# Projecting the image prompts' keys and values together in two 32-column weight tiles

## The chip, the cores and the metric

The kernel runs on one core of one Trainium2 chip. The metric is device time in microseconds (us) of one execution. Three runs of the kernel before took 433.48, 433.68 and 434.69 us; their median is 433.68 us. Engines are named as in the profile: PE is the matrix engine, PEld its weight loads, DVE the vector engine, ACT the scalar engine, POOL the general engine, and SP the engine whose queue issues the transfers (DMAs).

## The reference

There are 8 batches. In each, 112 query rows of 320 channels attend, with 20 heads of 16 channels, to a context of 375 rows of 512 channels. The last 4 rows of every context are image prompts; the other 371 are text.

```python
text_ehs = encoder_hidden_states[:, :-NUM_TOKENS]        # 371 rows
ip_ehs = encoder_hidden_states[:, -NUM_TOKENS:]          # 4 rows
q = heads(hidden_states @ W_q)
k_t, v_t = heads(text_ehs @ W_k), heads(text_ehs @ W_v)
probs_t = softmax(q k_t^T * attn_scale)
text_out = probs_t v_t
k_ip, v_ip = heads(ip_ehs @ W_k_ip), heads(ip_ehs @ W_v_ip)
attn_scores = q k_ip^T * attn_scale
qsem = l2norm(probs_t text_ehs);  sem = qsem l2norm(ip_ehs)^T
probs_ip = softmax(attn_scores + 0.5 * sem) * spatial_mask
out = (text_out + probs_ip v_ip) @ W_out + b_out + hidden_states
```

Only `k_ip` and `v_ip` concern the change: the 4 prompt rows of all 8 batches, 32 rows of 512 channels, times two weight matrices of 512 by 320. They are computed once for all batches.

## The kernel before

The 20 heads of a batch go in five steps of four heads. One batch has five steps, and `steps` lists all forty. The main loop goes through them in pairs (`pair`, or `alone` for the first), and after each pair `behind(n)` does what is left between: the Gram matrix, keys, values and queries of the next batch, and the end of the batch before. The order on PE, SP and DVE, and in the loop on ACT and POOL too, is the order in which the program is written. Nothing is moved by a planner.

A step runs like this. Scores (`ps_s`) are a product of keys `kT` and queries `qm` on PE, 32 channels of contraction for each head. DVE takes their maximum (`nmx`, L645), ACT the exponential (`p`, L649). SP's queue sends `p` to a rearranged buffer `xg` (L658), and DVE transposes 32x32 blocks of that into `xgT` (L672). PE multiplies `xgT` with the batch's matrix `u` into `ps_qd` (L683), four heads side by side, each in its own 32 rows of the array. ACT (L710) and DVE (L743) read the result. Scores are made two steps ahead: within the pair of steps 1 and 2, PE also makes those of step 3, in PSUM banks of the pools `sc` and `mm` (two banks each), and the first products of step 2 use these same four banks. So they wait until ACT's `p` of step 3 has read them.

PSUM banks come from three pools (`qd` 4, `sc` 2, `mm` 2 banks). `bank(name)` takes the pool that the list `turn` names next, and `behind` fills that list.

The prompts: `normalised_prompts` transposes the 32 prompt rows into `ipT` (128 partitions, 4 chunks of the contraction, 32 prompts). `wip` holds both prompt weight matrices; SP's queue loads them with `load_embed` behind the transfers of step 1, and then loads `x`, `W_out` and the bias. `prompt_projections` is a generator; `run` advances it piece by piece.

- L267, in `behind(0)`: `spread` on POOL (L123, L124) moves the last 64 of the keys' weight columns apart, so that each head of 16 channels is followed by 16 zeros.
- L268 to L278: for each of three blocks of 128 key channels, four matmuls (`ps_kip`) with the weights standing in the array (128x128) and the 32 prompts streaming through. ACT copies the result into `kip` (channels on partitions), and DVE makes `kipb`, keys masked by head, for batch 0.
- L285 to L292: four matmuls (`ps_vip`) the other way round: 32 prompts stand as weights in 32 columns, 320 value columns stream. ACT copies them into `vip`.
- L295, in `behind(2)`: `vip` goes to DRAM. Later batches fetch their four rows from there.

`kip` is read by POOL in `keys(b)` (L476), which puts the prompts' keys behind the text's keys, first for batch 1 in `behind(2)`. `kipb` is read by `prompt_logits` in `behind(4)`. `k3` is a buffer in which heads 16 to 19 stand 32 channels apart with zeros between; batch 1 uses it first in `behind(2)`, when its values are done.

On PE each float32 matmul of the program appears as two weight loads and two matmul instructions; a transpose appears as one of each.

Of the kernel before, what the change touches and what calls it, by code (L numbers as in the profile page):

```python
# [8 lines left out]
F32 = mybir.dt.float32  # L9
# [11 lines left out]
def kernel(  # L21
# [14 lines left out]
    nc = tc.nc  # L36
    P = 128
    B, S, C = x.shape
    T, E = ehs.shape[1:]
    H = HEADS  # L40
    D = C // H
# [3 lines left out]
    NE = E // P  # L45
    HC = P // D
    NC = (C + P - 1) // P
    CP = NC * P
    FULL = C // P
# [7 lines left out]
    N = B * NIP  # L57
# [18 lines left out]
    work = ctx.enter_context(tc.tile_pool(name="work", bufs=2))  # L76
# [6 lines left out]
    turn = []  # L83
    pools = {"mm": ps_mm, "sc": ps_sc, "qd": ps_qd}

    def bank(name, spare=False):

        tag = turn.pop(0) if turn else "sc" if spare else "mm"
        return pools[tag].tile([P, 512], F32, tag=tag, name=name)
# [12 lines left out]
    wv_sb = const.tile([P, NE, C + REST], F32, tag="wv_sb", name="wv_sb")  # L102

    wip = work.tile([P, UCOL], F32, tag="u", name="wip")
    wkip_sb = wip[:, : NE * CP].rearrange("p (e f) -> p e f", f=CP)
    wvip_sb = wip[:, NE * CP : NE * (CP + C)].rearrange("p (e f) -> p e f", f=C)
    wo_sb = const.tile([P, NC, C], F32, tag="wo_sb", name="wo_sb")
    ip_sb = const.tile([N, E], F32, tag="ip_sb", name="ip_sb")
    sm_sb = const.tile([S, 1], F32, tag="sm_sb", name="sm_sb")
# [9 lines left out]
    def spread(eng, t):  # L119

        v = t[:, :, FULL * P :].rearrange("p k (a r d) -> p k a r d", r=2, d=D)
        for a in (3, 2, 1):
            eng.tensor_copy(v[:, :, a, 0, :], v[:, :, a // 2, a % 2, :])  # L123
        eng.memset(v[:, :, :, 1, :], 0.0)  # L124
# [43 lines left out]
    ident = const.tile([P, P], F32, tag="ident", name="ident")  # L168
# [38 lines left out]
    k3 = const.tile([P, NT, GROUP, 2, D], F32, tag="k3", name="k3")  # L207
# [7 lines left out]
    ipT = const.tile([P, NE, N], F32, tag="ipT", name="ipT")  # L215
    ipnT = const.tile([P, NE, N], F32, tag="ipnT", name="ipnT")
    kip = const.tile([P, NC, N], F32, tag="kip", name="kip")

    kipb = const.tile([P, NC, HC, NIP], F32, tag="kipb", name="kipb")
    vipd = dram.tile([N, C], F32, tag="vipd", name="vipd", bufs=1)  # L220
# [43 lines left out]

    def prompt_projections():

        spread(nc.gpsimd, wkip_sb)  # L267
        for i in range(NC):  # L268
            ps = bank(f"ps_kip{i}")
            for e in range(NE):  # L270
                nc.tensor.matmul(
                    ps[:, :N],
                    wkip_sb[:, e, i * P : (i + 1) * P],
                    ipT[:, e, :],
                    start=(e == 0),
                    stop=(e == NE - 1),
                )
            nc.scalar.copy(kip[:, i, :], ps[:, :N])  # L278
            nc.vector.tensor_tensor(
                kipb[:, i],  # L280
                kip[:, i, :NIP].unsqueeze(1).to_broadcast([P, HC, NIP]),
                hmask.unsqueeze(2).to_broadcast([P, HC, NIP]),
                ALU.mult,
            )
            yield  # L285
        ps = bank("ps_vip")
        for e in range(NE):
            nc.tensor.matmul(
                ps[:N, :C], ipT[:, e, :], wvip_sb[:, e, :], start=(e == 0), stop=(e == NE - 1)
            )  # L290
        vip = work.tile([N, C], F32, tag="vip", name="vip", bufs=1)
        nc.scalar.copy(vip, ps[:N, :C])  # L292
        yield

        nc.sync.dma_start(vipd, vip)  # L295
        yield


# [165 lines left out]
    def gram_to_groups(b, blocks):  # L464

        for q in blocks:
            for a in range(GROUP):
                nc.sync.dma_start(
                    st[b]["u"][a * RG : (a + 1) * RG, q * GW : (q + 1) * GW],
                    ug[q * RG : (q + 1) * RG, :],  # L470
                )
# [543 lines left out]
    def run(key, make, pieces=1):  # L1015

        if key not in gens:
            gens[key] = make()
        for _ in range(pieces):
            next(gens[key], None)  # L1020
# [58 lines left out]
    def k(b, pieces=1):  # L1079
        run(("k", b), lambda: keys(b), pieces)  # L1080
# [104 lines left out]
    def behind(n):  # L1185

        b, g = steps[n]
        nb = b + 1
        two = steps[n + 1 : min(n + 3, len(steps) - NG + 1)]

        def tr(i):
            if i < len(two):
                transposed(*two[i], 0, BLK // (1 + i))

        if b % 2 == 0 and g == 0:
            if n == 0:
                turn[:] = ["sc", "sc", "mm", "qd", "qd", "qd", "qd", "mm"]
            else:
                turn[:] = ["qd"] * 4 + ["mm"]
                k(b)  # L1200
                f(b - 1)
                if b - 1 < B - 2:
                    prompt_values(b - 1)
            gr(nb)
            tr(0)
            gr(nb)
            if n:
                f(b - 1)
            gr(nb)
            if n == 0:  # L1210
                run(("pp",), prompt_projections, NC + 1)
            v(nb)
            tr(1)
            if n:
                f(b - 1, 2)
            load_next(b + 2)
        elif b % 2 == 0 and g == 2:
            turn[:] = ["qd"] * 6 + ["mm"]
            gram_to_groups(nb, (2,))
            k(nb)  # L1220
            q(nb, 3)
            tr(0)
            v(nb)
            q(nb)
            v(nb)
            if b == 0:
                run(("pp",), None)
            tr(1)
            values_to_dram(nb, nc.sync)
        elif b % 2 == 0:  # L1230
            new = nb < B - 1
            turn[:] = ["qd"] * (3 + (b > 0)) + (["qd", "mm", "mm"] if new else ["mm"])
            turned(b + 2)
            q(nb, 1 + (not new))
            if b > 0:
                f(b - 1)
            else:
                run(("t", b), lambda: prompt_logits(b))
            k(nb)
            tr(0)  # L1240
            if b > 0:
                f(b - 1)
            if new:
                gr(nb + 1, 3)
            tr(1)
            if b > 0:
                f(b - 1)
            load_next(b + 3)
            if new:
                f(b)  # L1250
                prompt_values(b)
        elif g == 1:
            turn[:] = ["qd"] * 4 + ["mm"]
            gram_to_groups(nb, (2,))
            q(b)
            k(b)
            k(nb)
            tr(0)
            f(b - 1)
            v(nb)  # L1260
            tr(1)
            v(nb)
            f(b - 1, 3)
            values_to_dram(nb, nc.sync, 0, 2)
            if b == B - 3:
                prompt_values_by_head()
        else:
            turn[:] = ["qd"] * 3 + ["sc"]
            v(nb)
            f(b - 1)  # L1270
            values_to_dram(nb, nc.sync, 2)
            tr(0)
            k(nb)
            f(b - 1, 2)
            tr(1)
            values_to_groups(nb)
        assert not turn, (b, g, turn)

    for n in range(0, len(steps) - NG, 2):
# [4 lines left out]
        b, g = steps[n]  # L1284
# [16 lines left out]
    b = B - 1  # L1301
# [12 lines left out]
    for g in range(NG):  # L1314
# [20 lines left out]
        if g < NG - 1:  # L1335

            n = GROUP - 1 if g <= LEAD else 1
# [89 lines left out]
```

## Time and profile before

| What | Before |
|---|---|
| Median of three runs | 433.68 us (433.48 to 434.69) |
| The profiled execution's own time | 434.62 us |
| Its span, first to last instruction | 432.9 us |
| PE busy | 423.2 us (98%) |
| DVE, ACT, POOL busy | 328.5, 190.7, 112.1 us |
| Mean granted PE clock over the span | 0.995 |

The profiled execution has 1.7 us outside its span. In the page, the second part cuts the span into 40 slices of 10.8 us. A row of the timeline gives start, duration, engine, line, operation, output<-input, shapes, the number of instructions merged, and in brackets the idle time ahead with what ended it. A PE shape such as `128*32` gives the rows and columns of the array in use, and `128x320` after it the partitions and streamed columns. A row of grouped instructions gives the busy time, in which overlaps count once, and the mean duration of one. The duration of a PE instruction includes the time until its result has left the array, so that a stream's own pace is read from starts.

### The profile page before, as it was taken

How to read it: one execution, taken by the hardware profiler on the slowest of the kernel's cores; microseconds unless marked ns; L12 is line 12 of the kernel's file. 1: busy time of each engine (PE TensorE's matmuls, PEld its weight loads, DVE VectorE, ACT ScalarE, POOL GpSimd, SP SyncE). 2: the span in 40 equal slices, each digit the busy share in tenths (PEclk: the TensorE clock that was granted, in tenths of full speed). 3: DMA queues.
4: the chain of work that ended last, by engine and by line, in shares of the span. 5: the costliest groups of instructions: out<-in, count | busy, mean ns of one | idle time of the engine just before them, and what ended most of it. 6: DMA issues, size and time to landing. Idle time of an engine off the chain costs nothing. (4 is left out here: it accounts for less than half of the span.)

```text
span 432.9 us, 12985 instructions
## 1 busy us (share of the span) xinstructions
PE 423.2 (98%) x5024; PEld 323.8 (75%) x5024; DVE 328.5 (76%) x687; ACT 190.7 (44%) x649; POOL 112.1 (26%) x270
## 2 busy tenths in 40 slices
PE   8999999999999999999999999999999999999986
PEld 8756677778686887778686887778776888776783
DVE  4045467797899897796889898787888897778884
ACT  2264123334553454333643464233633563346793
POOL 4302200012151234012142126002133226026440
PEclk9999899999999999999999999999999999999999
DMA  8669946487554566576744466575755436663300
GB/s 243 171 173 248 213 112 154 143 192 155 148 142 123 157 160 150 152 177 138 181 134 124 127 171 159 144 187 134 173 160 145 111 101 166 175 157 100 101 4 27
DMA packets 57931, 64.21 MB, mean 148 GB/s; under 512 B 18368, under 2 KB 52024, under 8 KB 57870
## 3 DMA queue, kind: packets, MB, share of 16 engines
q1 hardware_dynamic: 57304, 62.66, 57.2%
q8 instruction: 40, 0.66, 0.7%
q10 hardware_dynamic: 566, 0.72, 0.5%
q14 instruction: 21, 0.17, 0.1%
HBM read 18.67 MB, written 5.32 MB: 55 GB/s over the span
## 5 line engine op out<-in xcount | busy, mean ns | idle before, releaser
L683 PE MATMUL ps_qd<-u,xgT 32*112 32x232 f32 (+11 forms) x3840 | 215.4, 352 | 1.9 <-POOL u L599 1.9
L683 PEld LDWEIGHTS ps_qd<-u,xgT 32*112 32x112 f32 x3840 | 180.0, 172 | 36.5 <-issue 8.1
L672 DVE STREAM_TRANSPOSE xgT<-xg 128x768 f32<-128x768 f32 (+1 forms) x63 | 121.2, 1951 | 9.2 <-DMA xg<-p 9.1
L649 ACT ACTIVATE p<-ps_s,nmx 112x371 f32<-112x371 f32 x160 | 85.8, 586 | 52.5 <-DVE nmx L645 48.5
L743 DVE CUSTOM_DVE_ANT_0 junk<-ps_qd,p 112x371 f32<-112x371 f32 x148 | 80.2, 542 | 31.5 <-ACT pvs L710 11.4
L645 DVE TENSOR_REDUCE nmx<-ps_s 112x1 f32<-112x371 f32 x160 | 77.3, 537 | 28.0 <-PE ps_s L632 26.0
L599 POOL COPY u<-vr 128x64 f32<-128x64 f32 x120 | 26.7, 237 | 192.9 <-PE ps_qd L683 116.4
L526 PE MATMUL ps_v<-wv_sb,ctxT 128*128 128x384 f32 (+1 forms) x192 | 63.5, 477 | 0.3 <-ACT kT L499 0.3
L632 PE MATMUL ps_s<-kT,qm 32*112 32x375 f32 (+1 forms) x320 | 61.9, 487 | 1.0 <-ACT shared L728 0.7
L526 PEld LDWEIGHTS ps_v<-wv_sb,ctxT 128*128 128x128 f32 x192 | 35.4, 190 | 20.7 <-ACT kT L499 1.2
L710 ACT COPY pvs<-ps_qd 112x21 f32<-112x21 f32 x150 | 21.4, 200 | 62.2 <-DVE ss L743 61.0
L492 PE MATMUL ps_k<-ctxT,wk_sb 128*128 128x371 f32 x136 | 45.8, 481 | 0.0
L454 PE MATMUL ps_g<-ctxT 128*128 128x375 f32 (+2 forms) x168 | 36.8, 375 | 0.0
L454 PEld LDWEIGHTS ps_g<-ctxT 128*128 128x128 f32 x168 | 28.3, 191 | 8.7
L492 PEld LDWEIGHTS ps_k<-ctxT,wk_sb 128*128 128x128 f32 x136 | 24.6, 190 | 13.4 <-issue 0.5
L632 PEld LDWEIGHTS ps_s<-kT,qm 32*112 32x112 f32 x320 | 27.9, 171 | 6.9 <-ACT shared L728 1.3
L533 ACT COPY vext<-ps_v 128x384 f32<-128x384 f32 (+1 forms) x24 | 11.2, 466 | 37.1 <-PE ps_v L526 37.0
L651 ACT COPY ipl<-ps_s 112x4 f32<-112x4 f32 x140 | 24.2, 173 | 0.0
L443 ACT ACTIVATE ug<-ps_g 128x375 f32<-128x375 f32 (+2 forms) x24 | 9.0, 377 | 29.4 <-PE ps_g L454 20.5
L499 ACT COPY kT<-ps_k 128x371 f32<-128x371 f32 x17 | 8.0, 469 | 30.8 <-PE ps_k L492 30.8
L336 DVE TENSOR_SCALAR qm<-ps_q,emask 128x224 f32<-128x224 f32 (+1 forms) x25 | 8.9, 395 | 15.9 <-PE ps_q L327 15.9
L444 POOL TENSOR_TENSOR ug<-ug,half 128x128 f32<-128x128 f32 (+1 forms) x24 | 10.8, 448 | 35.3 <-ACT ug L443 35.0
(160 smaller groups left out, 333.5 us busy)
## 6 DMA issues: line engine op xcount, KB each, us to landing
xg<-p SPq DMA_DIRECT2D x159, 162.3 KB
u<-ug SPq DMA_DIRECT2D x128, 99.0 KB
ct<-in_ctx_dram SPq DMA_DIRECT2D x24, 176.0 KB
vr<-vd SPq DMA_DIRECT2D x32, 120.0 KB
vip<-vipd SPq DMA_DIRECT2D x6, 560.0 KB
vd<-vext SPq DMA_DIRECT2D x4, 480.0 KB
out_dram<-ob SPq DMA_DIRECT2D x8, 140.0 KB
ct<-in_ctx_dram SPq DMA_DIRECT2D x4, 256.0 KB
```

What stands on the lines that cost most here:

```text
L454: nc.tensor.matmul(ps[:, : T - t0], ctxT[:, e, t0 : t0 + P], ctxT[:, e, t0:T], start=(e == 0), stop=(e == NE - 1),)
L492: nc.tensor.matmul(ps[:, :TT], wk_sb[:, e, i * P : (i + 1) * P], s["ctxT"][:, e, :TT], start=(e == 0), stop=(e == NE - 1),)
L526: nc.tensor.matmul(ps[:, :w], ctxT[:, e, c * P : (c + 1) * P], wv_sb[:, e, :w], start=(e == 0), stop=(e == NE - 1),)
L599: nc.gpsimd.tensor_copy(region(b, c)[:, :, UV - c * P :], s["vr"][:, c * QN : (c + 1) * QN, g, :])
L632: nc.tensor.matmul(ps[:S, :w], qm[a * RG : (a + 1) * RG, i, r, j * S : (j + 1) * S], s["kT"][a * RG : (a + 1) * RG, i, :w], start=True, st ...
L645: nc.vector.tensor_reduce(nmx, ps[:S, :TT], AX.X, ALU.max, negate=True)
L649: nc.scalar.activation(p, ps[:S, :TT], AF.Exp, bias=nmx)
L651: nc.scalar.copy(s["ipl"][:, groups[g][a], :], ps[:S, TT:T])
L672: nc.vector.transpose(xT[:, j : j + n].rearrange("p j (k q) -> p q j k", q=QN), xg[:, :, j * RG : (j + n) * RG].rearrange("p q (j k) -> p ...
L683: nc.tensor.matmul(banks[a][:S, j * RG : UW], xT[a * RG : (a + 1) * RG, j, :S], region(b, c)[a * RG : (a + 1) * RG, q, q * RG :], start=(j ...
L710: nc.scalar.copy(s["pvs"][:, h, :], ps[:S, TT:UW])
L743: nc.vector.tensor_tensor_reduce(out=junk, in0=ps[:S, :TT], in1=s["p", g][:, a, :], scale=1.0, scalar=0.0, op0=ALU.mult, op1=ALU.add, accu ...
```

## The change

Both projections now have the 32 prompts standing as weights. The keys' matmuls write partitions 0 to 31 of one PSUM bank and so use array columns 0 to 31; the values' matmuls write partitions 32 to 63 and use columns 32 to 63. Key and value matmuls alternate. One ACT copy takes both (`kv`, 64x320). POOL copies the last 64 key columns from `kv` into rows 0 to 31 of `k3`, whose zeros stand already. Later, in `behind(2)` ahead of the keys of batch 1, PE transposes the three blocks of keys (`ps_kipT`), ACT copies them into `kip` in one instruction, and DVE makes `kipb` in three. `spread` is no longer called on the keys' weights, and these are loaded without gaps.

```diff
-    wkip_sb = wip[:, : NE * CP].rearrange("p (e f) -> p e f", f=CP)
-    wvip_sb = wip[:, NE * CP : NE * (CP + C)].rearrange("p (e f) -> p e f", f=C)
+    wkip_sb = wip[:, : NE * C].rearrange("p (e f) -> p e f", f=C)
+    wvip_sb = wip[:, NE * C : 2 * NE * C].rearrange("p (e f) -> p e f", f=C)
...
-        spread(nc.gpsimd, wkip_sb)
-        for i in range(NC):
-            ps = bank(f"ps_kip{i}")
-            for e in range(NE):
+        ps = bank("ps_kv")
+        for e in range(NE):
+            for i, w in enumerate((wkip_sb, wvip_sb)):
                 nc.tensor.matmul(
-                    ps[:, :N],
-                    wkip_sb[:, e, i * P : (i + 1) * P],
+                    ps[i * N : (i + 1) * N, :C],
                     ipT[:, e, :],
+                    w[:, e, :],
                     start=(e == 0),
                     stop=(e == NE - 1),
                 )
-            nc.scalar.copy(kip[:, i, :], ps[:, :N])
+        kv = work.tile([2 * N, C], F32, tag="vip", name="kv", bufs=1)
+        nc.scalar.copy(kv, ps[: 2 * N, :C])
+        k3p = k3[:N, 0]
+        nc.gpsimd.tensor_copy(
+            k3p[:, :, 0, :], kv[:N, FULL * P :].rearrange("n (a d) -> n a d", d=D)
+        )
+        yield
+
+        ps = bank("ps_kipT")
+        for i in range(NC):
+            nc.tensor.transpose(
+                ps[:, i * N : (i + 1) * N],
+                kv[:N, i * P : (i + 1) * P] if i < FULL else k3p.rearrange("n a r d -> n (a r d)"),
+                ident[:N, :N],
+            )
+        nc.scalar.copy(kip, ps[:, : NC * N].rearrange("p (i n) -> p i n", n=N))
+        for i in range(NC):
             nc.vector.tensor_tensor(
                 kipb[:, i],
...
-        ps = bank("ps_vip")
-        for e in range(NE):
-            nc.tensor.matmul(
-                ps[:N, :C], ipT[:, e, :], wvip_sb[:, e, :], start=(e == 0), stop=(e == NE - 1)
-            )
-        vip = work.tile([N, C], F32, tag="vip", name="vip", bufs=1)
-        nc.scalar.copy(vip, ps[:N, :C])
-        yield
-
-        nc.sync.dma_start(vipd, vip)
+        nc.sync.dma_start(vipd, kv[N:])
         yield
...
             if n == 0:
-                turn[:] = ["sc", "sc", "mm", "qd", "qd", "qd", "qd", "mm"]
+                turn[:] = ["sc", "sc", "mm", "qd", "mm"]
...
             if n == 0:
-                run(("pp",), prompt_projections, NC + 1)
+                run(("pp",), prompt_projections)
...
         elif b % 2 == 0 and g == 2:
-            turn[:] = ["qd"] * 6 + ["mm"]
+            turn[:] = ["qd"] * (6 + (b == 0)) + ["mm"]
             gram_to_groups(nb, (2,))
+            if b == 0:
+                run(("pp",), None)
             k(nb)
```

## The prediction

> **What bounds the kernel now.** I read the page first: the busy shares, and the clock in slices.
>
> ```profile
> span 432.9 us, 12985 instructions
> PE 423.2 (98%) x5024; PEld 323.8 (75%) x5024; DVE 328.5 (76%) x687; ACT 190.7 (44%) x649; POOL 112.1 (26%) x270
> PEclk9999899999999999999999999999999999999999
> ```
>
> PE is busy in 98% of the span, so a stage is worth what it occupies on PE, unless something else ends later there. One slice, the fifth (43 to 54 us), has a lower clock. That is where the prompt projections run. So next I took PE's timeline there, and then the granted clock in three stretches.
>
> ```profile
> 46.34 0.61 PE L454 MATMUL ps_g<-ctxT 128*128 128x119 f32 x4
> 46.79 1.88 PE L271 MATMUL ps_kip<-ipT,wip 128*128 128x32 f32 x16
> 48.90 1.08 PE L271 MATMUL ps_kip<-ipT,wip 128*128 128x32 f32 x8 [0.23 <-POOL wip L124]
> 49.91 4.03 PE L288 MATMUL ps_vip<-wip,ipT 128*32 128x320 f32 x8
> 53.87 2.85 PE L526 MATMUL ps_v<-wv_sb,ctxT 128*128 128x384 f32 x8
> 56.65 0.60 PE L683 MATMUL ps_qd<-u,xgT 32*112 32x392 f32 x4
> ```
>
> ```profile
> core 0: us, PE busy (x) PEld busy (x) DVE busy (x) ACT busy (x) POOL busy (x), PEclk, DMA share, GB/s
> 46.53:49.95 3.42, 3.19 (x29) 3.04 (x29) 1.34 (x3) 0.66 (x4) 1.93 (x7) 1.00 1.02 213
> 49.95:53.36 3.41, 3.41 (x8) 1.20 (x8) 0.19 (x1) 0.19 (x1) 0.00 (x0) 0.50 1.13 202
> 53.36:56.77 3.41, 3.41 (x14) 1.56 (x16) 1.56 (x1) 0.43 (x2) 0.00 (x0) 1.00 0.89 157
> ```
>
> The stage goes from the first `ps_kip` (46.79) to the first `ps_v` (53.87): 7.08 us, back to back. Its keys take 3.12 us: 24 instructions that stream only 32 columns each, paced by weight loads, and one wait for POOL's spreading. Its values take 3.96 us, and for 3.41 us of that the clock was granted at 0.50. The stretch before it, of the same length, is the one filled with the keys' short streams.
>
> What the values cost at full clock follows from as many instructions with the same 320 columns elsewhere:
>
> ```profile
> L288 PEld LDWEIGHTS ps_vip<-wip,ipT x8: 125/177/178, 49.9 to 53.1; 128*32 128x32 f32 x8
> L288 PE MATMUL ps_vip<-wip,ipT x8: 433/741/741, 49.9 to 53.5; 128*32 128x320 f32 x8
> 13.25 2.33 PE L526 MATMUL ps_v<-wv_sb,ctxT 128*128 128x320 f32 x8
> 15.41 0.45 PE L319 MATMUL ps_x<-ident,x_sb 112*128 112x112 f32 x3
> ```
>
> Eight take 15.41 - 13.25 = 2.16 us, 0.27 us each. The last `ps_vip` starts at 53.5, and `ps_v` at 53.87: 0.1 us more than its own 0.27, to empty the array before the tile shape changes. So the values cost about 2.26 us at full clock, and the half clock 1.7 us. Two of the runs took near 433.6 us and one 434.69, like the profiled execution's 434.62. I suppose, without being able to see it, that the faster ones had no half clock. So I make the sum twice: against 434.62, and against 433.6 with a stage of 7.08 - 1.70 = 5.38 us. The Trainium skill ("TensorE: Matmul & The Clock Gate", Part 1) says that the clock halves after a window of some 3.4 us with little work on PE, and that these windows run freely; the trace's 3.41 us agrees, and by that rule executions would differ so.
>
> **The change, step by step.**
>
> *The new matmuls.* 16 instructions of 320 columns, 32 array columns each, alternating by pairs between two column tiles. Before has no two column tiles at work together. The lower bound is that they run abreast: 8 x 0.27 = 2.16 us. The upper bound for streaming alone is one after another: 16 x 0.27 = 4.32 us. The nearest row is that of the row tiles, with a lone full-width stream beside it:
>
> ```profile
> L683 PE MATMUL ps_qd<-u,xgT 32*112 32x296 f32 x320 | 29.4, 408 | 0.0
> L526 PE MATMUL ps_v<-wv_sb,ctxT 128*128 128x320 f32 x48 | 13.9, 436 | 0.3 <-ACT kT L499 0.3
> ```
>
> 320 instructions of 408 ns fill only 29.4 us, 92 ns each, so four row tiles do run abreast; the full-width ones fill 290 ns each. I take the lower bound for column tiles, and keep both ends. With 0.1 us for the change of array shape at each end, the stage is 2.36 us.
>
> *Weight loads.* There are 16, of 32 columns. By the `ps_vip` rows above a load takes 0.18 us, and loads and streams of one column tile start together (both at 49.9, the last at 53.1 and 53.5), while PE's timeline has no gap: loads lie under streams, so I count nothing. If that cover went, 16 x 0.18 = 2.9 us would come on top, and with streams one after another the stage would be 4.32 + 2.88 + 0.2 = 7.4 us, a rival below. The Trainium skill ("TensorE: Matmul & The Clock Gate", Part 3) speaks against the change here: a weight load overlaps a running matmul only where their row groups differ, and these tiles share all rows. By that rule the stage would be those 7.4 us instead of 2.36; the trace disagrees for one column tile.
>
> *So PE reaches `ps_v` earlier* by 7.08 - 2.36 = 4.72 us against the profiled execution, 3.02 us against one at full clock. The wait for POOL (0.23 us) is in it. POOL's spreading and three of ACT's four copies go too; nothing else waited for them.
>
> *What is late next.* PE's next steps need scores of step 3 to be worked off, and DVE is in order:
>
> ```profile
> 54.59 1.56 DVE L672 STREAM_TRANSPOSE xgT<-xg 128x768 f32<-128x768 f32 x1 [4.16 <-DMA xg<-p]
> 58.23 1.90 DVE L645 TENSOR_REDUCE nmx<-ps_s 112x1 f32<-112x371 f32 x4 [2.08 <-PE ps_s L632]
> 60.04 1.59 DVE L672 STREAM_TRANSPOSE xgT<-xg 128x768 f32<-128x768 f32 x1
> 58.81 1.96 ACT L649 ACTIVATE p<-ps_s,nmx 112x371 f32<-112x371 f32 x4 [1.58 <-DVE nmx L645]
> L683 PE MATMUL ps_qd<-u,xgT 32*112 32x392 f32 x2 | 0.5, 497 | 0.0
> L683 PE MATMUL ps_qd<-u,xgT 32*112 32x392 f32 x4 | 0.9, 527 | 0.0
> ```
>
> The last two rows are groups of the stretches 61.5 to 61.6 and 61.88 to 61.90: streams of 392 columns open a step, so step 2's products begin near 61.57 and, for its other two heads, 61.89. They take the banks from which `p` of step 3 is read until 58.81 + 1.96 = 60.77: 1.1 us of slack. But `nmx` stands on DVE behind a transpose that waits for a transfer landing at 54.59. PE doesn't move that transfer. The queue that brings it is full:
>
> ```profile
> 38.00:40.60 2.60, 2.60 (x52) 2.13 (x48) 1.81 (x4) 1.95 (x4) 0.24 (x1) 1.00 0.94 256
> 40.60:42.60 2.00, 2.00 (x47) 1.64 (x40) 0.55 (x2) 0.41 (x4) 0.48 (x2) 1.00 1.01 392
> 48.00:54.60 6.60, 6.37 (x24) 3.26 (x24) 0.59 (x4) 0.79 (x3) 0.87 (x5) 0.74 1.09 196
> wip<-in_L_xattn_W_k_ip_dram SPq DMA_DIRECT2D x1, 640.0 KB
> ```
>
> The share of the DMA engines (the column before GB/s) is about 1 up to the landing. The keys' weights now go in whole rows like the values' weights, without gaps: 640 KB at 256 GB/s (the stretch where I place the keys' load) would take 2.6 us, at 392 GB/s (the values') 1.7 us. I take 0.6 us, nearer to the rows' 0.9 than to 0, since not all of the slower stretch need be this load. Then the transfer lands at 54.0, the transpose ends at 55.56, and `nmx` starts there, not at 58.23 - 4.72 = 53.51. That is 2.67 us earlier than before; `p` ends at 58.10. PE would want the banks at 61.89 - 4.72 = 57.17, waits 0.98 us with 0.05 us for the signal, and has gained 3.74 us. Against an execution at full clock the gain is 3.74 - 1.70 = 2.04 us. Without a faster transfer it is 0.6 us less; without any such wait 0.98 us more.
>
> *The transposes* in `behind(2)`, three on PE ahead of batch 1's keys. Four of the same shape:
>
> ```profile
> 7.13 0.66 PE L257 MATMUL ps_ipTn<-ident,ipn 32*128 32x32 f32 x4
> 7.63 0.64 PE L257 MATMUL ps_ipTr<-ident,ip_sb 32*128 32x32 f32 x4
> L278 ACT COPY kip<-ps_kip 128x32 f32<-128x32 f32 x3 | 0.6, 186 | 2.3 <-PE ps_kip L271 2.3
> L279 DVE TENSOR_TENSOR kipb<-kip,hmask 128x32 f32<-128x32 f32 x3 | 0.6, 192 | 2.4 <-ACT kip L278 2.4
> L292 ACT COPY vip<-ps_vip 32x320 f32<-32x320 f32 x1 | 0.4, 415 | 3.8 <-PE ps_vip L288 3.8
> 74.66 0.81 DVE L336 TENSOR_SCALAR qm<-ps_q,emask 128x224 f32<-128x224 f32 x2 [0.76 <-PE ps_q L327]
> 67.74 0.20 POOL L476 COPY kT<-kip 128x12 f32<-128x12 f32 x1
> 68.00 0.28 POOL L310 MEMSET xT<- 64x224 f32 x1
> 73.33 1.30 PE L327 MATMUL ps_q<-xT,wq_sb 128*128 128x224 f32 x6
> 51.94 2.76 SPq L143 DMA_DIRECT2D ct<-in_ctx_dram  x4
> 59.41 3.58 SPq L658 DMA_DIRECT2D xg<-p  x4
> ```
>
> 7.63 - 7.13 = 0.5 us for four, 0.38 us for three, all on PE's path. Their inputs are long ready, with `kv` (ACT, 0.4 us) and its POOL copy done soon after the stage. `kipb` moves on DVE to before step 3's transpose: 0.6 us, which the 0.76 us idle ahead of `qm` covers; without that cover 0.6 us. POOL's L476 now waits for ACT's `kip`, and behind it stands the clearing of `xT`, which PE needs only 5 us later (73.33): nothing. POOL's new copy into `k3` waits for `kv`, and behind it a clearing of `ct` for which the transfers L143 wait; SP has nothing behind these before 59.41, so up to 4 us are free. The values' own transfer keeps its place on SP.
>
> *Sum.* Against the profiled execution: -3.74 + 0.38 = -3.36 us, 434.62 to 431.3. Against full clock: -2.04 + 0.38 = -1.66 us, 433.6 to 431.9. The second holds for more runs if two of three were such; I take 431.6, between them.
>
> **The rivals.**
> *One stream at a time* (for: both tiles read the same partitions; against: the row tiles). Stage 4.52 us, 2.56 us earlier, `nmx` no longer blocked: -2.18 and -0.48 us, 432.4 and 433.1; say 432.8, no measurable change.
> *Weight loads bared* (for: the two tiles share all rows, which no row tiles do; against: the `ps_vip` rows). Stage 7.4 us: +0.32 + 0.38 = +0.7 from 434.62, 2.02 + 0.38 = +2.4 from 433.6; 435.3 to 436.0, say 435.6, slower. It decides when 16 instructions take over (5.38 - 0.38 - 0.2) / 16 = 0.30 us each.
> *The half clock stays*, now on the new matmuls or behind them, since a quarter or half of the columns might count as little work (against: the values alone, in 32 columns, ended the half-clock stretch at 53.36). 1.7 us more, of which 0.98 us falls into the wait for DVE: 431.6 + 0.7 = 432.3.
>
> **How the numbers follow.** About 0.3%, 1.3 us, is what the runs (433.48 to 434.69) can tell from no change; faster begins under 432.4. Abreast 0.58, one at a time 0.20, bared loads 0.12, half clock 0.10. Faster: 0.55 of the first (0.03 for a later transfer) and half of the last, 0.60. Slower: bared loads, and 0.04 of one at a time, for tiles that slow each other beyond 0.30 us, 0.16. Same: what is left, 0.24. The low end is the gain without a DVE wait against full clock: 433.6 - 3.02 + 0.38 = 431.0, less 0.2; the high end is one at a time against full clock, 433.1, plus 0.2. The likeliest case's own range is 430.8 to 432.5.
>
> **What would show it.** `ps_kv` with 16 instructions in about 2.3 us; about 4.4 us, or 7.3, would be the first or second rival. No slice but the last at half clock. Before step 2's products, PE waiting about 1 us for ACT's `p`; DVE still waiting for `xg`, landing near 54.0. Three `ps_kipT` in 0.4 us, and `ps_k` after them with no new wait. I'm wrong if column tiles share the stream, or if the transfer lands later than before.

## The result

| | Before | After |
|---|---|---|
| Median | 434.13 us (6 executions, 433.48 to 434.89) | 432.11 us (6, 431.63 to 432.89) |
| Ratio | | 0.9955 (95%: 0.994 to 0.997) |
| The profiled execution's own time, and its span | 434.62, 432.9 us | 431.93, 430.2 us |

The changed kernel is 2.0 us faster. In a later comparison with more executions, `after_again` below, the ratio was 0.9977 (434.48 to 433.10 us), a smaller gain; the experiments show what the rest depends on.

The first part of the page of after, and its clock in slices, answer to the lines shown of before:

```profile
span 430.2 us, 12955 instructions
PE 420.1 (98%) x5011; PEld 322.3 (75%) x5011; DVE 328.3 (76%) x687; ACT 190.0 (44%) x647; POOL 111.1 (26%) x267
PEclk9999999999999999999999999999999999999999
```

PE is busy for 3.1 us less, and the slice at reduced clock is gone. The timeline of the prompt stage and of what follows (after's lines lie 7 further down: `ps_qd` is L690, `nmx` L652, `p` L656, `xgT` L679):

```profile
46.27 2.35 PE L270 MATMUL ps_kv<-wip,ipT 128*32 128x320 f32 x16
48.55 2.85 PE L533 MATMUL ps_v<-wv_sb,ctxT 128*128 128x384 f32 x8
51.32 1.22 PE L690 MATMUL ps_qd<-u,xgT 32*112 32x392 f32 x10
53.91 1.57 DVE L679 STREAM_TRANSPOSE xgT<-xg 128x768 f32<-128x768 f32 x1 [7.06 <-DMA xg<-p]
55.33 1.83 DVE L652 TENSOR_REDUCE nmx<-ps_s 112x1 f32<-112x371 f32 x4
55.85 1.95 ACT L656 ACTIVATE p<-ps_s,nmx 112x371 f32<-112x371 f32 x4 [3.94 <-DVE nmx L652]
56.56 3.81 PE L690 MATMUL ps_qd<-u,xgT 32*112 32x392 f32 x49 [0.16 <-ACT p L656]
```

The two groups of `ps_kv` by tile (minimum, median, maximum ns of one; first and last start):

```profile
L270 PEld LDWEIGHTS ps_kv<-wip,ipT x16: 106/110/110, 46.3 to 47.9; 128*32 128x32 f32 x16
L270 PE MATMUL ps_kv<-wip,ipT x16: 432/432/457, 46.3 to 48.2; 128*32 128x320 f32 x16
```

Both projections take 48.55 - 46.27 = 2.28 us instead of 7.08. Then DVE's transpose is 7.06 us idle for the transfer of step 2's `p`, `nmx` starts behind it without a gap, `p` behind that, and PE's first products of step 2 end a wait for `p`.

Where the 4.7 us went is best read from the times between the first products of 392 columns of successive steps (steps 1 and 2 of after begin at 51.32 and 56.56 above). The start varies by 2 us between executions, whatever the kernel (the last section shows why), so the table counts from step 0 (first products at 36.26 us in before, 35.64 in after):

| From, to | Before | After | Difference |
|---|---|---|---|
| step 0 to 1 (prompt stage) | 20.39 | 15.68 | -4.71 |
| step 1 to 2 | 4.92 | 5.24 | +0.32 |
| step 2 to 3 | 15.57 | 16.58 | +1.01 |
| step 3 to 24 | 201.46 | 201.46 | 0 |
| step 24 to 25 | 16.59 | 17.56 | +0.97 |
| step 25 to the end of the span | 137.71 | 138.05 | +0.34 |

The first three rows sum to -3.38 us. Of the +1.33 us in rows two and three, 0.17 are the transposes in `behind(2)`, seen below without any wait, and 1.16 are the wait for `p`. Of that wait only the 0.16 us ahead of 56.56 stand in these rows as idle time; the rest is a difference between the two traces, and `loads_later` below shows that all of it goes when the transfer is early. The last two rows give back 1.3 us more, over 200 us after the change; together with a start 0.62 us earlier that is the 2.7 us between the spans.

### The profile page after: what moved, and what is told of

The parts are those of the page before. It is cut to its first block, busy times and chain, and to the rows that moved or that the text cites. A ratio compares the mean times of both kernels' runs of the same rounds, so it can differ in the third digit from the quotient of the medians.

```text
span 430.2 us, 12955 instructions
## 1 busy us (share of the span) xinstructions
PE 420.1 (98%) x5011; PEld 322.3 (75%) x5011; DVE 328.3 (76%) x687; ACT 190.0 (44%) x647; POOL 111.1 (26%) x267
## 5 line engine op out<-in xcount | busy, mean ns | idle before, releaser
L690 PE MATMUL ps_qd<-u,xgT 32*112 32x104 f32 (+11 forms) x3840 | 216.8, 352 | 2.0 <-POOL u L606 1.7
L690 PEld LDWEIGHTS ps_qd<-u,xgT 32*112 32x112 f32 x3840 | 182.0, 172 | 35.8 <-issue 8.0
L679 DVE STREAM_TRANSPOSE xgT<-xg 128x768 f32<-128x768 f32 (+1 forms) x63 | 121.2, 1952 | 12.3 <-DMA xg<-p 12.2
L656 ACT ACTIVATE p<-ps_s,nmx 112x371 f32<-112x371 f32 x160 | 85.6, 585 | 54.8 <-DVE nmx L652 53.2
L652 DVE TENSOR_REDUCE nmx<-ps_s 112x1 f32<-112x371 f32 x160 | 77.2, 535 | 26.7 <-PE ps_s L639 24.7
```

The costliest lines, as they stand in the source:

```text
L652: nc.vector.tensor_reduce(nmx, ps[:S, :TT], AX.X, ALU.max, negate=True)
L656: nc.scalar.activation(p, ps[:S, :TT], AF.Exp, bias=nmx)
L679: nc.vector.transpose(xT[:, j : j + n].rearrange("p j (k q) -> p q j k", q=QN), xg[:, :, j * RG : (j + n) * RG].rearrange("p q (j k) -> p ...
L690: nc.tensor.matmul(banks[a][:S, j * RG : UW], xT[a * RG : (a + 1) * RG, j, :S], region(b, c)[a * RG : (a + 1) * RG, q, q * RG :], start=(j ...
```

## The experiments

Each kernel is compared with the kernel before on one chip, run side by side. There were four such comparisons behind the first result, each on another chip, with medians of before of 434.48 us (beside `after_again`, `same_tile`, `loads_later` and `gapped`), 433.80 (beside `mixed_before`, `before_later` and `loads_later_2`), 434.04 (beside `warm_tail` and `later_warm`) and 434.89 (beside `later_warm_2`). Beside medians I use each execution's mean granted PE clock, since one stretch of 3.41 us at 0.50 takes 0.004 off it. The three groups are executions with no such stretch, with one, and with two, apart from the last 4 us of the span. Over all chips they are (number, median us):

| Kernel | Clock 0.998 to 1.0 | 0.994 to 0.996 | 0.992 or less |
|---|---|---|---|
| Before (beside all experiments) | 30, 433.63 | 52, 434.60 | 3, 437.22 |
| The changed kernel (first result and `after_again`) | 13, 432.33 | 1, 434.21 | 4, 434.81 |
| `same_tile` | 11, 433.08 | 1, 433.39 | 0 |
| `gapped` | 3, 433.19 | 6, 434.90 | 3, 436.98 |
| `mixed_before` | 7, 433.84 | 2, 434.41 | 3, 436.45 |
| `before_later` | 4, 433.68 | 7, 434.45 | 1, 437.20 |
| `loads_later` and `loads_later_2` | 9, 430.57 | 1, 432.34 | 8, 434.01 |
| `warm_tail` | 11, 432.60 | 0 | 0 |
| `later_warm` | 6, 431.41 | 0 | 0 |
| `later_warm_2` | 6, 431.20 | 0 | 0 |

**The changed kernel again** (no edit).

> The changed kernel once more, unedited, for a second trace and more times. Theory: the stage `ps_kv` is 2.27 us again, 16 streams abreast in two column tiles, no half clock before the end of the span, and PE waits about 1.1 us in all for ACT's `p` of step 3 behind a transfer that lands near 53.9. The two later losses against before in the first trace (0.97 us at step 25, where PE waited for POOL behind a late transfer of the values, and 0.37 us near step 30) are scatter of single transfers: the trace has them elsewhere or not at all, and the median is 432.1 us within 0.5. Rival: they belong to the change, shifted transfers that collide; then both come back at the same steps with the same size.

Measured: 433.10 us (12 executions, 431.14 to 435.60), ratio 0.9977 (0.9957 to 0.9997): less of a gain than expected. In the profiled execution the stage took 2.28 us again, with no half clock, and PE waited longer:

```profile
47.82 2.35 PE L270 MATMUL ps_kv<-wip,ipT 128*32 128x320 f32 x16
50.10 2.85 PE L533 MATMUL ps_v<-wv_sb,ctxT 128*128 128x384 f32 x8
52.88 1.22 PE L690 MATMUL ps_qd<-u,xgT 32*112 32x392 f32 x10
55.86 1.57 DVE L679 STREAM_TRANSPOSE xgT<-xg 128x768 f32<-128x768 f32 x1 [7.44 <-DMA xg<-p]
58.52 1.86 PE L690 MATMUL ps_qd<-u,xgT 32*112 32x392 f32 x19 [0.56 <-ACT p L656]
```

The transpose starts 2.98 us after step 1's first products (2.59 in after), and the wait is 1.56 us instead of 1.16. Step 24 to 25 took 17.22 us, 0.63 over before where after had 0.97, and from step 25 on nothing is lost (137.69 us): neither reading of the expectation fits both losses. The stage, the wait and the missing half clock repeat; the median doesn't, because 5 of the 12 executions lie at a clock of 0.992 to 0.995 and take 434.2 us or more. The other seven have a median of 432.39.

**Two column tiles against one.** Keys and values both in columns 0 to 31, in two banks and with two ACT copies; the same matmuls in the same order.

```diff
-        ps = bank("ps_kv")
+        pss = [bank("ps_kv"), bank("ps_kv2")]
...
-                    ps[i * N : (i + 1) * N, :C],
+                    pss[i][:N, :C],
...
-        nc.scalar.copy(kv, ps[: 2 * N, :C])
+        nc.scalar.copy(kv, pss[0][:N, :C])
+        nc.scalar.copy(vv, pss[1][:N, :C])
...
```

> The changed kernel with keys and values in the same array columns 0 to 31, in two banks and with two ACT copies, so that no two column tiles work together. Theory: 16 streams one after another, 16 x 0.27 = 4.3 us, stage 4.4 instead of 2.27 us, so PE is 2.15 us later at step 1; but the 1.1 us wait for step 3's `p` is gone, since the transfer that holds DVE lands as before: 1.05 us slower than the changed kernel, 433.2 us. Rival 1: loads show between the streams, 16 x 0.45 = 7.2 us, 436 us. Rival 2: the wait follows PE and not the transfer, so that it stays: 2.15 us slower, 434.3 us.

Measured: 433.13 us (432.14 to 434.29), ratio 0.9967 (0.9952 to 0.9982). PE in that execution:

```profile
47.85 4.49 PE L270 MATMUL ps_kv<-wip,ipT 128*32 128x320 f32 x16
52.27 2.85 PE L535 MATMUL ps_v<-wv_sb,ctxT 128*128 128x384 f32 x8
56.63 1.90 DVE L654 TENSOR_REDUCE nmx<-ps_s 112x1 f32<-112x371 f32 x4 [1.34 <-PE ps_s L641]
```

The stage takes 52.27 - 47.85 = 4.42 us, 2.14 more: in one column tile the sixteen run one after another at 0.27 us, in two tiles by pairs. But `nmx` now waits for PE's scores and not for the transfer; PE waits nowhere, and the 1.2 to 1.6 us of wait are gone. Among executions at full clock, 433.08 against 432.33: of 2.1 us that the second tile saves on PE, 0.75 us arrive. Letting the prompts stand as weights, with one column tile, is worth 0.55 us by the same measure (433.63 to 433.08).

This execution had a half clock from 28.90 to 32.32 us, which put step 0 some 1.7 us later while the transfer came as ever: its transpose starts 16.52 us after step 0, or 18.2 without that. In after, step 2's products were held until 3.5 us after that transpose began (51.32 + 4.92 + 1.16 - 53.91). Here that would be 18.2 + 3.5 = 21.7 us after step 0, and step 2 comes at 22.75: PE would not have waited without the half clock either.

**The loads behind the late transfer.** On SP's queue the loads of `x`, `W_out`, the mask and the bias move from ahead of step 2's `xg<-p` to behind it.

```diff
     load_embed(nc.sync, wvip_sb, w_v_ip)
-    nc.sync.dma_start(x_sb[:, 1:5, :], x[1:5].rearrange("b s c -> s b c"))
-    load_channels(nc.sync, wo_sb, w_out)
-    nc.sync.dma_start(sm_sb, smask.unsqueeze(1))
...
             alone(n)
+            nc.sync.dma_start(x_sb[:, 1:5, :], x[1:5].rearrange("b s c -> s b c"))
+            load_channels(nc.sync, wo_sb, w_out)
+            nc.sync.dma_start(sm_sb, smask.unsqueeze(1))
...
```

> The changed kernel with the loads of `x`, `W_out`, the mask and the bias issued on SP behind the transfers of step 2's `p` instead of ahead of them. Theory: the transfer that holds DVE at 53.9 lands before 48, DVE's `nmx` of step 3 starts with PE's scores, PE's wait of 1.1 us before and in step 2's first products goes: 1.1 us faster than the changed kernel, 431.0 us, step 2 opening 4.92 us after step 1 as before. Rival 1: the loads now collide with the transfers of step 3 or of the next context, and PE waits there instead: no gain, 432.1 us or more. Rival 2: the wait comes from DVE's and ACT's own work, not from the transfer: unchanged at 432.1 us.

> The kernel of loads_later, again, with more rounds. Theory (the wait of 1.0 to 1.5 us for the late transfer is gone, and nothing else of it changes): 430.4 us +- 0.4, ratio 0.991 to 0.993 to the kernel before. Rival (the 430.47 of the first runs was a chance): nearer to the 432 to 433 us of the changed kernel.

Measured first: 430.47 us (6 executions, 429.91 to 433.67), ratio 0.9919 (0.9894 to 0.9944). Again: 433.72 us (12, 430.51 to 434.91), ratio 0.997 (0.9947 to 0.9994). DVE in the first profile:

```profile
44.02 4.67 DVE L679 STREAM_TRANSPOSE xgT<-xg 128x1536 f32<-128x1536 f32 x2
53.06 1.90 DVE L652 TENSOR_REDUCE nmx<-ps_s 112x1 f32<-112x371 f32 x4 [4.38 <-PE ps_s L639]
```

Step 2's transpose follows the earlier one without a wait for the transfer (two merged at 44.02), and `nmx` waits for PE. Steps 1 to 2 and 2 to 3 take 4.92 and 15.74 us in both profiles: no wait, and 0.17 us over before for the three transposes. So the wait was the transfer's, and the transfer was late because these loads stood ahead of it. Among executions at full clock the gain over the changed kernel is 432.33 - 430.57 = 1.8 us. The second expectation's rival came out for the median, though, since 8 of the 18 executions lie at 0.992, with a median of 434.0 us.

**The same loads moved in the kernel before.**

> The kernel before, with the loads of x, W_out, the mask and the bias issued behind the exchange of step 2's probabilities instead of ahead of it, which is all that loads_later has over the changed kernel. Theory (in the kernel before, the late transfer hides under 1.1 us of slack when the half clock falls, and costs about 0.6 us when it doesn't): DVE's transpose of step 2 starts near 48.5 without a wait for the transfer; executions with the half clock stay at 434.6, those without come to 432.9; median near 434.3, ratio 0.998 to 1.000. Rival (the loads cost the kernel before as much as the changed one): 1.6 us faster, 432.8.

Measured: 434.18 us (433.44 to 437.2), ratio 1.0005 (0.9987 to 1.0023): no gain. The executions at full clock take 433.68 us, as before's do (433.63), and not the 432.9 of the theory. The profiled execution had no half clock; step 0 to 1 took 18.70 us, and PE waited for nothing behind the transfer. So it became worth moving only when the stage ahead of it became short.

**The keys' weights with gaps.** The layout of before, and so the same DMA rows, under the new matmuls.

```diff
-    wkip_sb = wip[:, : NE * C].rearrange("p (e f) -> p e f", f=C)
-    wvip_sb = wip[:, NE * C : 2 * NE * C].rearrange("p (e f) -> p e f", f=C)
+    wkip_sb = wip[:, : NE * CP].rearrange("p (e f) -> p e f", f=CP)[:, :, :C]
+    wvip_sb = wip[:, NE * CP : NE * (CP + C)].rearrange("p (e f) -> p e f", f=C)
```

> The changed kernel with the keys' weights loaded with gaps as before (rows of 384 columns of which 320 are filled), nothing else. Theory: the load takes 0.5 to 0.6 us longer on full DMA engines, so the transfer of step 2's `p` lands near 54.5 instead of 53.9 and the wait on PE grows by as much: 0.55 us slower than the changed kernel, 432.65 us. Rival: the layout costs nothing on the way to that landing: landing at 53.9, 432.1 us.

> The kernel of gapped, one more profile, to see where its executions at 0.992 to 0.996 have their half clock. Theory: at the end (6.83 us, 3.1 us lost, clock 0.992) or, with 0.995, in one window of 3.41 us somewhere ahead of it, either near 28 us as in same_tile or where PE waits for p before step 2 (near 56 us); 434.3 to 437 us. Rival: no half clock but late transfers.

Measured: 434.9 us (12 executions, 431.97 to 438.34), ratio 1.0018 (0.9993 to 1.0042); the second profile's execution took 431.78 us. The transposes of the two profiles:

```profile
54.80 1.57 DVE L679 STREAM_TRANSPOSE xgT<-xg 128x768 f32<-128x768 f32 x1 [7.36 <-DMA xg<-p]
```
```profile
54.99 1.57 DVE L679 STREAM_TRANSPOSE xgT<-xg 128x768 f32<-128x768 f32 x1 [7.27 <-DMA xg<-p]
```

Counted from step 0 (36.21 and 36.49) the transpose starts at 18.59 and 18.50 us. In the changed kernel it starts at 18.27 (after), 18.66 (`after_again`) and 18.60 (`warm_tail`), in the kernel before at 18.33 and 18.48 (`before_again`). Whole rows without gaps bring the transfer no earlier. The wait is 1.39 to 1.49 us, as in the changed kernel, so the rival describes the traces. The median fits neither, being over both. Neither profiled execution had a half clock ahead of the last 3 us. Nine of the twelve timed ones lie at 0.996 or less, and where those lost 2 to 6 us no profile shows: that stays open.

**What the half clock costs the kernel before.** One more profile of it, and a kernel in which the value matmuls stand in portions between the key blocks.

```diff
+            if pv is None:
+                pv = bank("ps_vip")
+            for e in ((0, 1), (2,), (3,))[i]:
+                nc.tensor.matmul(
+                    pv[:N, :C], ipT[:, e, :], wvip_sb[:, e, :], start=(e == 0), stop=(e == NE - 1)
+                )
             yield
-        ps = bank("ps_vip")
-        for e in range(NE):
-            nc.tensor.matmul(
...
```

> The kernel before, unchanged, one more profile. Its timed runs fall into two groups: granted clock 0.998 or above (medians near 433.5 us) and 0.995 to 0.996 (near 434.6 us). Theory: the groups differ by the half-clock stretch of 3.41 us near 50 us and by nothing else, and it is the run of 24 narrow key streams that brings it. If this execution has it, step 0 to step 1 takes 20.4 us and step 1 to step 2 4.9 us; if not, 18.7 us and 5.5 us: the wait for ACT's p of step 3 then takes back 0.6 us of the 1.7, and the difference between the groups is 1.1 us, as timed. Rival: without the stretch the 1.7 us would be kept whole, and the two groups' 1.05 us has another origin.

> The kernel before, with the eight value instructions (320 columns) no longer behind the 24 key instructions (32 columns) but in three portions between them. The same work, in another order. Theory (the clock is halved after a stretch filled with narrow streams alone): no half clock near 50 us, all runs at a clock of 0.998 or more, step 0 to 1 about 18.9 us (18.7 plus 0.1 for each of two more changes of array shape), the wait of step 2 for p about 0.5 us; median 433.6 to 433.9 us, ratio 0.998. Rival (the stretch comes from elsewhere, from work before 46.8 us): the same two groups as before, median 434.4.

Measured: `before_again` 434.34 us; `mixed_before` 433.96 us (433.34 to 438.25), ratio 1.0009 (0.9984 to 1.0035). Stretches around the stage (length; busy us and instructions of PE, PEld, DVE, ACT and POOL; clock; DMA share; GB/s), first `before_again`, then `mixed_before`:

```profile
46.03:49.44 3.41, 3.18 (x30) 3.07 (x28) 1.62 (x3) 0.95 (x4) 1.93 (x7) 1.00 1.00 223
49.44:52.86 3.42, 3.42 (x9) 1.45 (x9) 0.19 (x1) 0.19 (x1) 0.00 (x0) 0.50 1.12 195
```
```profile
46.89:50.30 3.41, 3.41 (x21) 2.12 (x20) 0.84 (x3) 0.64 (x3) 1.54 (x7) 1.00 1.03 215
50.30:53.71 3.41, 3.41 (x16) 2.16 (x16) 0.21 (x2) 0.60 (x2) 0.00 (x0) 1.00 1.16 206
```

With the same work in another order the half clock near 50 us is gone: step 0 to 1 takes 18.74 us instead of 20.33, and only 2 of 12 executions lie at 0.994 to 0.996, against 52 of 85 of before. So it was the unbroken run of narrow key streams that brought it. My expectation that a wait for `p` then takes back 0.6 us was wrong: step 1 to 2 takes 4.92 us in `mixed_before`, with no wait. The groups of before differ by 0.97 us and not by the 1.6 of the traces, and no profile caught an execution of before at full clock. But the traces suggest where the other 0.6 us goes: ahead of step 0. Rows of PE at the start of before and of `before_later` (whose profile had no half clock near 50 us):

```profile
4.49 1.35 PE L414 MATMUL ps_w<-ident 128*128 128x128 f32 x6
5.68 0.63 PE L397 MATMUL ps_c<-ident,ct 128*128 128x128 f32 x4
7.13 0.66 PE L257 MATMUL ps_ipTn<-ident,ipn 32*128 32x32 f32 x4
```
```profile
4.66 1.48 PE L414 MATMUL ps_w<-ident 128*128 128x128 f32 x6
5.93 1.06 PE L397 MATMUL ps_c<-ident,ct 128*128 128x128 f32 x4
7.85 0.66 PE L257 MATMUL ps_ipTn<-ident,ipn 32*128 32x32 f32 x4
```

The same four transposes `ps_c` take 0.63 us in one and 1.06 in the other. In the trace the record of the granted clock begins at 5.57 us in before, 5.07 in `before_again` and 6.93 in `before_later`, and PE works at about half its pace ahead of that (its instructions of 128 columns start 0.21 us apart there, and 0.11 to 0.12 behind it). Step 0 follows at 36.26, 36.06 and 36.77 us. So the two executions that met the half clock near 50 us started 0.5 to 0.7 us sooner, which is about the missing amount; three traces don't prove it for the groups. And the median of `mixed_before` isn't better than before's, because 3 of its 12 executions lie at 0.992.

**The end of the kernel.** The profile of `loads_later_2` caught such an execution. Its last 21 us, from step 39's first products, and the same stretch of `loads_later`:

```profile
411.65:416.34 4.69, 4.69 (x94) 4.69 (x95) 3.55 (x15) 4.19 (x16) 1.58 (x4) 1.00 0.00 0
416.34:419.75 3.41, 2.88 (x29) 2.14 (x24) 3.12 (x12) 3.28 (x10) 0.33 (x1) 1.00 0.00 0
419.75:426.58 6.83, 6.83 (x18) 4.13 (x17) 2.66 (x16) 2.71 (x7) 0.00 (x0) 0.50 0.01 2
426.58:432.65 6.07, 2.59 (x10) 1.16 (x8) 0.98 (x2) 0.50 (x2) 0.00 (x0) 1.00 0.16 47
```
```profile
410.31:414.41 4.10, 4.09 (x68) 4.08 (x72) 3.09 (x13) 3.63 (x14) 1.27 (x3) 1.00 0.00 0
414.41:417.82 3.41, 2.94 (x52) 2.58 (x45) 3.01 (x12) 3.35 (x10) 0.63 (x1) 1.00 0.00 0
417.82:424.65 6.83, 6.83 (x30) 3.76 (x28) 3.70 (x19) 3.60 (x10) 0.00 (x0) 1.00 0.08 23
```

For 6.83 us, two windows, the clock is 0.50, and the end takes 21.00 us instead of 17.87: 3.13 us. `mixed_before` shows the same in its profile (21.01 us). To see whether this makes the executions at 0.992, two kernels, the changed one and `loads_later`, got a product that nobody reads, near PE's 0.5 us wait in this stretch.

```diff
+            warm = ps[:S, S : S + C]
             ps = bank(f"ps_a_{b}_{h0}")
             for i in range(i0, i1):
...
+                if b == B - 2 and i == 0:
+                    nc.tensor.matmul(warm, ident[:S, :S], attn[:, :C], start=True, stop=True)
...
```

> The changed kernel with one more product on PE near the end, whose result nobody reads: 112 rows, 320 columns (two instructions, 0.54 us), placed in the 0.52 us in which PE waits there for ACT's copies. Theory: the executions at a granted clock of 0.992 lose 3.1 us at the end of the kernel, because a window of 3.41 us that begins about 4.4 to 5.3 us after the last step's first product holds only 1.9 us of streams, and the 6.83 us after it are granted at 0.50. The filler makes that 2.5 us. So no execution at 0.992, the stretch from the last step's first product to the end takes 17.9 to 18.0 us, and the median is 432.2 us with all runs between 431.5 and 433.2; ratio 0.994 to 0.997. Rival: the 0.992 comes from elsewhere; a quarter or more of the runs stay at it, above 434 us.

> The kernel of loads_later (x, W_out, mask and bias issued behind the exchange of step 2) with the same filler at the end. Theory as for warm_tail: of loads_later's two groups, 430.5 to 431.1 us at full clock and 433.6 to 434.9 us at 0.992, only the first is left; median 430.6 us, ratio 0.991 to 0.993. Rival: both groups stay, median 432 to 434.

Measured: `warm_tail` 432.6 us (431.85 to 433.79), ratio 0.9963 (0.995 to 0.9976); `later_warm` 431.41 us (430.95 to 431.81), ratio 0.9933 (0.9916 to 0.9949). Both medians are 0.4 and 0.8 us above what was expected, and one run of `warm_tail` 0.6 above its bound, but none of these 17 executions lies under 0.998, and none over 433.8 us. In 49 executions of the changed kernel, `gapped` and `loads_later` 15 lie at 0.992. These 15 come from two other comparisons, on other chips; on the chip of the filler one execution without it was timed, `gapped_again`, at 1.0. So the counts alone don't exclude that the chips differ. The filler cost more than expected, as PE in `later_warm` shows:

```profile
417.08 0.47 PE L850 MATMUL ps_a<-ident,attn 112*128 112x112 f32 x2
418.08 0.79 PE L854 MATMUL ps_wT<-attn,ident 112*112 112x320 f32 x2 [0.52 <-ACT bT L936]
418.71 0.37 PE L855 MATMUL ps_a<-wT,bd 80*128 80x112 f32 x2
```

It stands behind the wait and not in it, since it writes a bank that ACT is still reading; the end takes 18.38 us, 0.5 more. The clock in this profile is of more weight than the counts:

```profile
416.56:419.97 3.41, 2.89 (x22) 2.22 (x20) 3.12 (x13) 2.80 (x9) 0.16 (x1) 1.00 0.00 0
419.97:423.39 3.42, 3.42 (x17) 2.15 (x16) 2.47 (x15) 2.83 (x7) 0.00 (x0) 1.00 0.02 5
```

A window begins here 4.86 us after step 39's first products, between the 4.69 us of `loads_later_2` and the 5.23 of `mixed_before`, and no half clock follows. The reason that the expectation gives is not shown, though. The filler pushes later products out of this window, which then holds no more streams than that of `loads_later_2` (1.9 against 2.0 us, counted at 0.27 us for 320 columns). The last kernel, `loads_later` again, has the filler ahead of the wait, in unused columns of the next bank.

```diff
             ps = bank(f"ps_a_{b}_{h0}")
+            if b == B - 2:
+                warm = ps[:S, NC * S : 512]
+                for c in range(2):
+                    part_c = attn[:, c * 176 : c * 176 + 176]
+                    nc.tensor.matmul(warm, ident[:S, :S], part_c, start=True, stop=True)
...
```

> As later_warm, but the filler (two products of 176 columns, four instructions) goes into unused columns of the bank that PE fills next, and stands ahead of the wait for ACT's copies, not behind it. In later_warm it stood behind the wait, since it wrote a bank that ACT was reading, and cost 0.53 us. Theory: the same protection, in cover; no run at 0.992, the stretch from the last step's first product to the end 17.9 us, not 18.4; 430.4 to 431.2 us, ratio 0.992. Rival: the filler still pushes back what follows, or does not raise the window's streaming enough; 431.4 us, or some runs at 0.992 above 433.

Measured: 431.2 us (6 executions, 430.71 to 432.49), ratio 0.9913 (0.989 to 0.9935), none under a clock of 0.999, the end 17.87 us. Its profile too has a window from 4.86 us after step 39's first products, with 2.5 us of streams and no half clock behind it. This is the lowest ratio of all kernels, though its interval overlaps with those of `later_warm` and of the first six executions of `loads_later`. Its median is 0.2 us under `later_warm`'s, not 0.5, with a start 0.8 us later in its profile (step 0 at 37.53 against 36.72); which filler is better isn't settled by six executions each on two chips.

## Why the prediction was right, and where its steps were not

The time (431.6 us predicted, 432.11 measured) and the sign were right, and the profile shows the likeliest case. That the time came so near is in part luck, as the last three points show.

- *The stage.* 2.28 us against 2.36 predicted. `same_tile` shows that the second column tile makes half of it. *One stream at a time* describes `same_tile`, not the changed kernel, and its time was right for it: 432.8 predicted, 433.1 measured.
- *Weight loads.* At nothing, right: PEld's 16 loads of 0.11 us start while streams run, and the stage is 8 x 0.27 + 0.1 us. (The prediction's 0.18 us for a load was read from rows at half clock.) The rule of the Trainium skill ("TensorE: Matmul & The Clock Gate", Part 3) that a load overlaps only in other row groups doesn't hold here: these share all rows. (The same section also names loads into a background weight buffer as pulled ahead; these rows agree with that.)
- *What is late next.* Right in place and mechanism, and `loads_later` shows it by taking the transfer's delay away. The size was 1.16 to 1.56 us, not 0.98. The failed term is the 0.6 us that the transfer was to gain from rows without gaps (without it the prediction's own sum gives 1.58): counted from step 0 the transpose starts at 18.3 to 18.7 us in both layouts. (Two profiles lie lower, `mixed_before` at 18.02 and `same_tile`, whose step 0 was late, at 16.52.) In the first profile its absolute start (53.91, near the predicted 54.0) only seemed to confirm it, since that execution began 0.62 us earlier.
- *The transposes.* 0.17 us, not 0.38: three start within 63.05 to 63.33 us. `kipb` (0.39 us) hid in DVE's idle time as said, 0.73 us ahead of `qm`.

```profile
63.05 0.28 PE L287 MATMUL ps_kipT<-ident,kv 32*128 32x32 f32 x2
63.33 2.76 PE L499 MATMUL ps_k<-ctxT,wk_sb 128*128 128x371 f32 x8
66.65 0.39 DVE L294 TENSOR_TENSOR kipb<-kip,hmask 128x32 f32<-128x32 f32 x3
```

- *The sum.* To the end of the change's reach, step 3, the trace gives -3.38 us against -3.36: by errors that cancel (0.18 us more wait, 0.21 us less transposing). Behind that, 1.3 us were given back at places that the sum didn't name, the largest ahead of a Gram matrix after step 24 (POOL and PE in after):

```profile
286.64 0.19 POOL L380 COPY ctxT<-ipnT 128x16 f32<-128x16 f32 x1
286.89 2.47 PE L461 MATMUL ps_g<-ctxT 128*128 128x375 f32 x7 [0.70 <-POOL ctxT L380]
```

POOL copies late there because it waited 9.9 us for transfers. From step 24 to 25 PE takes 16.59 us in before, `before_again` and `before_later`, and 16.58 to 17.56 in the eleven other profiles. That these transfers don't always come earlier when PE does is what this suggests; no run tested it.
- *Two kinds of executions of before.* That the faster ones have no half clock is what the clock groups show. The difference is 0.97 us, not 1.7. So the pairs as timed are -1.3 us between executions at full clock (433.63 to 432.33), where -1.66 was predicted, and -2.3 from a half-clock execution of before (434.60), where -3.36 was. At full clock the steps account for it roughly: the stage saves 3.02 us (18.70 in `before_later` to 15.68), and 1.16 to 1.56 of wait, 0.17 of transposes and up to 0.97 ahead of step 25 go off.
- *The half clock stays.* Not on the new matmuls in any of the profiles of the changed stage. But the rival's form was too narrow: to judge by the clock, the changed kernel pays 3.1 us at the end in 4 of 18 executions, and before in 3 of 85 (the end itself was seen in the profiles of `loads_later_2` and `mixed_before` alone). In the first result it didn't occur, and the prediction's right number owes something to that.

Why before is spared at the end is argued, not shown. The windows run freely against the kernel. In the two profiles with a slow end a window began 4.69 and 5.23 us after step 39's first products; with 4.32 (`same_tile`) and 5.35 (after) the end took 17.86 us, and with 3.56 (before) and 3.31 (`before_again`) 17.88 and 17.85. Before's half clock near 50 us comes only for some positions of the windows, and then shifts the end by 1.6 us against them. That would leave positions at the end that before hardly reaches. `mixed_before`, which only takes away the half clock near 50 us, has a slow end in 3 of 12 executions, as this asks for.

## What to carry to other kernels

When a stage gets shorter, look up which transfer was landing under it: here the second column tile saved 2.1 us on PE and 0.75 us arrived, until the loads ahead of that transfer on the queue were moved. Compare executions by their granted clock before comparing medians: a change that removes one half-clock stretch can expose another, and a median then measures how often each is met. None of the 23 executions with a small product in the thin stretch of PE met that chance, and placed ahead of a wait that is there anyway the product cost nothing (an end of 17.87 us); why it helps is open.

## What the runs showed that was not expected

- The half clock has two places in this program, each behind a window of 3.41 us in which PE looks busy in the profile (93% and 84%) but streams little: counted at 0.27 us for 320 columns, 1.0 to 1.1 us near 47 us in before and 2.0 us near the end. Streams alone don't decide it: after has a window with the same 2.0 us, from 417.69, and `later_warm` the one with 1.9 us shown above, both with the clock at 1.00 behind them, and `before_later` one with 1.6 us from 47.89. The exact condition stays open. `same_tile` shows a third place, 28.9 to 32.3 us, once.
- All boundaries of the granted clock in one execution lie whole multiples of 3.413 us apart (in before 49.95 and 432.24: 382.29 us, 112 windows), and where they lie against the program differs from execution to execution. The Trainium skill ("TensorE: Matmul & The Clock Gate", Part 1) says the same, that the window of 3413 ns runs freely.
- These windows also set the start. The record of the granted clock begins between 4.68 us (after; step 0 at 35.64) and 8.08 us (`later_warm_2`; 37.53), with PE at about half pace ahead of it, and by and large step 0 comes later the later it begins. Of the 0.62 us by which after's profiled execution reached step 0 sooner than before's, 0.43 stand already at the prompts' first transposes (`ps_ipTn` at 6.70 against 7.13 us), ahead of all that the change touches on PE.
- Two column tiles with all 128 rows in common stream abreast: 16 instructions of 320 columns in 2.28 us, against 4.42 us in one column tile.
